# A two-layer 5x5 convolution: from 4-row to 6-row Winograd tiles, with part of the input transform on GpSimd and pair sums kept in PSUM

## The chip, the cores and the metric

The kernel runs on one core of one Trainium2 chip. The metric is device microseconds of one execution of the program. A core has five engines that run their own instruction queues in order: TensorE (PE in the profile; PEld is its loading of weights), VectorE (DVE), ScalarE (ACT), GpSimd (POOL) and SyncE (SP), which here only issues DMAs. Data lies in DRAM, in SBUF (128 partitions) and in PSUM, where TensorE writes its products.

## The reference

Two layers, each adding to x a 5x5 convolution of the group-normalised x (reflect padding, 16 groups of 2 channels, mean and variance over the group's pixels):

```python
def _gn(v, G=16, eps=1e-5):
    g = v.reshape(B_, G, C_ // G, H_, W_)
    m = jnp.mean(g, axis=(2, 3, 4), keepdims=True)
    s = jnp.var(g, axis=(2, 3, 4), keepdims=True)
    return ((g - m) / jnp.sqrt(s + eps)).reshape(v.shape)

x = x + _L0_conv_ref(_gn(x), L0_conv_weight)
x = x + _L1_conv_ref(_gn(x), L1_conv_weight)
```

x is (8, 32, 252, 252) in fp32, the weights are (32, 32, 5, 5). The convolution is written with an FFT in the reference; it is an ordinary 5x5 convolution with reflected borders.

## The kernel before

**Layout.** Pixels are grouped into 2x2 blocks. A partition is one of 4 positions in the block times 32 channels, 128 in all, and an image becomes 126x126 blocks, padded to 128x128. The 5x5 convolution is then a 3x3 convolution over blocks with 128 input and 128 output partitions.

**Winograd along block rows.** Along the rows of blocks the kernel uses F(4,3): 4 output rows from 6 input rows, by 6 products instead of 12. Along the columns it does the 3 taps directly, as 3 matmuls that accumulate. A step takes a group of 16 block rows as NT = 4 tiles of TR = 4 rows; the last group of an image has 14 real rows. There are NG = 8 groups to an image, 2 layers and 8 images, so 128 steps. Phases go (image 0, layer 0), then in turn (b, layer 0) and (b-1, layer 1).

**One step.**
- `fetch` (SP) loads the raw rows of a group of layer 0 into one half of `xbuf`. `prepare` makes g, the group's 18 block rows with their padding: for layer 0 with two big ScalarE copies (L131) and three small ones, for layer 1 with one DMA from `scratch` (L126).
- `transform` (VectorE) makes the six inputs v0 to v5 of the products from g: ab (L333), v1 and v2 (L342, L343), c (L345), v3 and v4 (L346, L347), and v0 and v5 in one tile (L349).
- `conv` runs six products, each 3 matmuls of 504 columns (4 tiles of 126) into one PSUM bank (L375), in the order 1, 2, 3, 4, 0, 5. ScalarE copies products 1 and 3 to SBUF (a1 with the offset, L390; a3, L398), so that each VectorE instruction has one operand in PSUM. VectorE forms s1 and d1 (L394, L395) and s2 and d2 (L402, L403), in SBUF, and from these the 4 rows of y (L404, L405, L408 to L412).
- y of the step before goes out during this step: for layer 0 `to_scratch` (padding copies, DMAs) and `output_sums` (two ScalarE activations that sum), for layer 1 `to_output` (four ScalarE copies L451, DMAs).

**Statistics and matrices.** `input_chunk` and `input_sums` sum the next image's input in 8 chunks; `collect`, `averages`, `variance`, `scales` make the group norm; `scale_matrices` scales the layer's matrices u by it on ScalarE, `add_own` adds the residual x (an identity) to them on VectorE, and `find_offset` makes the bias. The unscaled matrices of both layers stay in SBUF; they are made at the start by `load_taps`, `transform_taps` (GpSimd, L167 to L178) and `make_matrices` (ScalarE, L200).

**Order.** The schedule is by hand: each engine executes its instructions as the program emits them. In iteration i of the main loop come: fetch of step i+3, chunk loads, variance and collect where due, `transform` of step i+1, scales where due, then `conv` of step i with `after_1` (prepare of step i+2), `after_3` (output of step i-1, chunk sums) and `after_4` (add_own). So VectorE runs transform(i+1), conv(i), transform(i+2), conv(i+1) and so on. Tiles rotate over a fixed number of buffers in each pool: a new tile waits until the last user of the tile whose buffer it takes has ended; `ps_conv` has 7 PSUM banks.

Of the kernel before, what the change touches and what calls it, by code (L numbers as in the profile page):

```python
# [42 lines left out]
P = 128  # L44
# [4 lines left out]
TR = 4  # L49
NT = 4  # L50
GR = TR * NT
NG = PB // GR
NF = 6
# [3 lines left out]
def tile_conv_preact_x2(ctx: ExitStack, tc: tile.TileContext, x: bass.AP, w0: bass.AP, w1: bass.AP, out: bass.AP):  # L57
# [7 lines left out]
    prep = ctx.enter_context(tc.tile_pool(name="prep", bufs=1))  # L65
    upool = ctx.enter_context(tc.tile_pool(name="upool", bufs=2))
    xpool = ctx.enter_context(tc.tile_pool(name="xpool", bufs=1))
    spool = ctx.enter_context(tc.tile_pool(name="spool", bufs=3))
    gpool = ctx.enter_context(tc.tile_pool(name="gpool", bufs=2))
# [4 lines left out]
    opool = ctx.enter_context(tc.tile_pool(name="opool", bufs=1))  # L74
    small = ctx.enter_context(tc.tile_pool(name="small", bufs=3))
    dram = ctx.enter_context(tc.tile_pool(name="dram", bufs=3, space=bass.MemoryType.DRAM))
    ps_conv = ctx.enter_context(tc.tile_pool(name="ps_conv", bufs=7, space=bass.MemoryType.PSUM))
    ps_stat = ctx.enter_context(tc.tile_pool(name="ps_stat", bufs=1, space=bass.MemoryType.PSUM))
# [10 lines left out]
    xbuf = xpool.tile([P, GR + 2, W], F32, tag="x", name="x")  # L89
    fetched = 0  # L90

    def fetch(b: int, l: int, T: int):
# [4 lines left out]
        nr = min(GR + 2, PB - GR * T)  # L97
        half = fetched % 2
        fetched += 1
        for pr in range(2):  # L100
            t = xbuf[quads[2 * half + pr]]

            runs, pads = [], []
            for k in range(nr):
                h = 2 * (GR * T + k) + pr - 1
                if 0 <= h < H:
                    runs.append(k)
                else:
                    pads.append((k, {-1: 1, H: H - 2, H + 1: H - 3, H + 2: 2}[h]))
            first = 2 * (GR * T + runs[0]) + pr - 1  # L110
            nc.sync.dma_start(
                t[:, runs[0] : runs[-1] + 1, :], x[b, :, first : first + 2 * len(runs) - 1 : 2, :]
            )
            for k, h in pads:
                nc.sync.dma_start(t[:, k, :], x[b, :, h, :])
        xt[b, T] = xbuf[halves[half]]

    def prepare(b: int, l: int, T: int):

        nr = min(GR + 2, PB - GR * T)  # L120
        g = gpool.tile([P, GR + 2, PB], F32, tag="g", name=f"g_{b}_{l}_{T}")
        gt[b, l, T] = g
        if nr < GR + 2:
            nc.gpsimd.memset(g[:, nr:, :], 0.0)
        if l:
            nc.sync.dma_start(g[:, :nr, :], scratch[b][:, GR * T : GR * T + nr, :])  # L126
            return
        t = xt.pop((b, T))
        h0, h1 = halves
        for pc in range(2):  # L130
            nc.scalar.copy(g[halves[pc], :nr, 1 - pc : 1 - pc + NB], t[:, :nr, 1 - pc : W : 2])  # L131
        nc.scalar.copy(g[h0, :nr, 0 : PB : PB - 1], g[h0, :nr, 1 : NB : NB - 2])
        for dst, src in ((126, 125), (127, 1)):
            nc.scalar.copy(g[h1, :nr, dst : dst + 1], g[h1, :nr, src : src + 1])  # L134
# [3 lines left out]
    raw, total = [], []  # L138

    def load_taps(l: int, w: bass.AP):  # L140

        t = prep.tile([P, 2, 3, K, C], F32, tag=f"taps{l}", name=f"taps{l}")
        nc.vector.memset(t, 0.0)
        for pc in range(2):
            for pr in range(2):
                for rp in range(2):
# [4 lines left out]
                    nc.scalar.dma_start(  # L151
                        t[quad(pc, pr), rp, lo : lo + n], w[:, first : first + 2 * n - 1 : 2, :, :]
                    )
        return t

    def transform_taps(l: int, t: bass.AP):

        r = prep.tile([P, NF, 2, K, C], F32, tag="rows", name=f"rows{l}")
        s = prep.tile([P, 2, K, C], F32, tag="rsum", name=f"rsum{l}")
# [6 lines left out]

# [3 lines left out]
        v.tensor_scalar(both(1), both(1), -1.0 / 6, None, ALU.mult)  # L170
        v.tensor_scalar(rf[0], t2, 4.0, None, ALU.mult)
        v.tensor_add(rf[0], rf[0], t0)
        v.tensor_scalar(rf[5], t1, 2.0, None, ALU.mult)
        v.tensor_add(rf[3], rf[0], rf[5])
        v.tensor_sub(rf[4], rf[0], rf[5])
        v.tensor_scalar(both(3), both(3), 1.0 / 24, None, ALU.mult)
        v.tensor_scalar(rf[0], t0, 0.25, None, ALU.mult)
        v.tensor_copy(rf[5], t2)  # L178
        return r

    def sum_taps(l: int, t: bass.AP):

        sums = prep.tile([P, C], F32, tag="sums", name=f"sums{l}")
        nc.vector.tensor_reduce(sums, t.rearrange("p r a k o -> p o (r a k)"), axis=AX.X, op=ALU.add)
        tot = const.tile([P, 4, C], F32, tag=f"total{l}", name=f"total{l}")
        for q in range(4):
            nc.vector.tensor_scalar(tot[:, q, :], sums, 0.25, None, ALU.mult)
        total.append(tot.rearrange("p q o -> p (q o)"))

    def make_matrices(l: int, r: bass.AP):  # L190
        u = const.tile([P, NF, 3, 2, 2, C], F32, tag=f"u{l}", name=f"u{l}")
        nc.gpsimd.memset(u, 0.0)
        for pc in range(2):
            for cp in range(2):
# [4 lines left out]
                for rp in range(2):  # L199
                    nc.scalar.copy(  # L200
                        u[halves[pc], :, lo : lo + n, 1 - cp, 1 - rp, :],
                        r[halves[pc], :, rp, first : first + 2 * n - 1 : 2, :],
                    )
        raw.append(u.rearrange("p f b c r o -> p (f b c r o)"))
# [4 lines left out]
    def make_own():  # L209
        coef = ((1 / 4, -1 / 6, -1 / 6, 1 / 24, 1 / 24, 0.0), (0.0, -1 / 6, 1 / 6, 1 / 12, -1 / 12, 0.0))  # L210
        for pc in range(2):
            for pr in range(2):
                for f in range(NF):
                    nc.gpsimd.tensor_scalar(
                        own[quad(pc, pr), f, :], ident[quad(pc, pr), halves[pc]], coef[1 - pr][f], None, ALU.mult
                    )
# [5 lines left out]
    def make_averages():  # L222
        for l, pattern in enumerate(("p (q g e) -> p g q e", "p (g q e) -> p g q e")):
            kinds = {"q": 4, "e": 2}
            member = const.tile([P, C // 2], F32, tag=f"member{l}", name=f"member{l}")
            nc.vector.tensor_reduce(member, ident.rearrange(pattern, **kinds), axis=AX.XY, op=ALU.add)
            nc.vector.tensor_scalar(member, member, 1.0 / COUNT, None, ALU.mult)
            a = const.tile([P, 4, C // 2, 2], F32, tag=f"avg{l}", name=f"avg{l}")
            for q in range(4):
                for e in range(2):  # L230
                    nc.gpsimd.tensor_copy(a[:, q, :, e], member)
            avg.insert(0, a.rearrange("p q g e -> p (q g e)"))
# [4 lines left out]
    def sum_slots(b: int, l: int):  # L237
        if (b, l) not in sums:
            sums[b, l] = small.tile([P, 2, NG], F32, tag="sums", name=f"sums_{b}_{l}")
# [17 lines left out]
    def output_sums(b: int, T: int, y: bass.AP):  # L257
        rows = min(GR, NB - GR * T)
        st = sum_slots(b, 1)
        view = y[:, 0 : rows * PB].rearrange("p (r k) -> p r k", k=PB)[:, :, 1 : 1 + NB]  # L260
        junk = spool.tile([P, GR, NB], BF16, tag="junk", name=f"junk_{b}_{T}", bufs=1)
        nc.scalar.activation(junk[:, :rows], view, AF.Identity, accum_out=st[:, 0, T : T + 1])  # L262
        nc.scalar.activation(junk[:, :rows], view, AF.Square, accum_out=st[:, 1, T : T + 1])  # L263
# [6 lines left out]
    def averages(b: int, l: int):  # L270

        pm = ps_stat.tile([P, 2], F32, tag="pstat", name=f"pm_{b}_{l}")
# [29 lines left out]
    ut, offset = {}, {}  # L302

    def scale_matrices(b: int, l: int, first: bool = False):
        u = upool.tile([P, NF, 3, P], F32, tag="u", name=f"u_{b}_{l}")
        flat, r = u.rearrange("p f b m -> p (f b m)"), norm[b, l][:, 0:1]
        if first:
            nc.vector.tensor_scalar(flat, raw[l], r, None, ALU.mult)
        else:
            nc.scalar.activation(flat, raw[l], AF.Identity, scale=r)  # L310
        ut[b, l] = u
# [6 lines left out]
    def find_offset(b: int, l: int):  # L318
        po = ps_stat.tile([P, 1], F32, tag="pstat", name=f"po_{b}_{l}")
# [5 lines left out]
    vt = {}  # L325

    def transform(b: int, l: int, T: int):
        g = gt.pop((b, l, T))
        n = f"{b}_{l}_{T}"
        v = nc.vector  # L330
        ab = apool.tile([P, NT, TR, PB], F32, tag="ab", name=f"ab_{n}")
        flat = ab.rearrange("p t r k -> p (t r k)")
        v.scalar_tensor_tensor(  # L333
            flat,
            g[:, 0:GR, :].rearrange("p r k -> p (r k)"),
            -4.0,
            g[:, 2 : GR + 2, :].rearrange("p r k -> p (r k)"),
            ALU.mult,
            ALU.add,
        )  # L340
        vs = [vpool.tile([P, NT, PB], F32, tag=f"v{k}", name=f"v{k}_{n}") for k in range(1, 5)]
        v.tensor_add(vs[0], ab[:, :, 2, :], ab[:, :, 1, :])  # L342
        v.tensor_sub(vs[1], ab[:, :, 2, :], ab[:, :, 1, :])  # L343
        c = apool.tile([P, NT, 2, PB], F32, tag="c", name=f"c_{n}")
        v.tensor_sub(c.rearrange("p t r k -> p t (r k)"), rows_of(g, 3), rows_of(g, 1))  # L345
        v.scalar_tensor_tensor(vs[2], c[:, :, 0, :], 2.0, c[:, :, 1, :], ALU.mult, ALU.add)  # L346
        v.scalar_tensor_tensor(vs[3], c[:, :, 0, :], -2.0, c[:, :, 1, :], ALU.mult, ALU.add)  # L347
        v05 = vpool.tile([P, NT, 2, PB], F32, tag="v05", name=f"v05_{n}")
        v.tensor_sub(  # L349
            v05.rearrange("p t r k -> p t (r k)"),  # L350
            ab[:, :, 2:4, :].rearrange("p t r k -> p t (r k)"),
            ab[:, :, 0:2, :].rearrange("p t r k -> p t (r k)"),
        )
        vt[b, l, T] = [v05[:, :, 0, :], *vs, v05[:, :, 1, :]]

    def rows_of(g: bass.AP, j: int):

        return g[:, j - 1 : j - 1 + GR, :].rearrange("p (t r) k -> p t r k", r=TR)[:, :, 1:3, :].rearrange(
            "p t r k -> p t (r k)"
        )  # L360
# [236 lines left out]
```

## Time and profile before

| what | value |
|---|---|
| time, median of 3 runs | 2029.58 us (2028.38 to 2029.70) |
| profiled execution | 2029.54 us, of which the span from first to last instruction is 2027.8 us |
| granted TensorE clock, mean | 0.997 |
| VectorE, largest groups | ab L333 292.2 us in 128, 2283 ns each; v0 and v5 L349 156.5 us, 1223 ns each |
| ScalarE, largest groups | o L451 283.3 us in 256; g L131 290.2 us in 128 |
| GpSimd | work in the start only, and 16 memsets of 0.31 us later |
| DMA | 346.77 MB, mean 171 GB/s |
| first matmul of a product | at 54.96 us |

A group of the page is a line of the program with an engine and an operation: the total busy time, the mean duration of one in ns, the idle time of the engine just before them and what ended it. The timeline gives start, duration, engine, line, operation, output <- inputs. Records of neighbouring instructions on one engine may overlap; so the distance from start to start tells what an instruction costs its engine.

### The profile page before, as it was taken

The numbers are of one execution on the slowest core, as the hardware profiler recorded it, in microseconds if no ns is written. First come the engines' busy times: TensorE is split into PE (matmuls) and PEld (weight loads), VectorE is DVE, ScalarE is ACT, GpSimd is POOL, SyncE is SP. The second block draws the span as 40 slices with busy tenths as digits, with TensorE's granted clock in tenths as the row PEclk, the third lists the DMA queues.
The fourth block names the chain that finished last, engine by engine and source line by source line (L and its number), as shares of the span: only waits on it lengthen the run. The fifth ranks groups of instructions, "written<-read, shape, count | busy, mean of one in ns | idle before, by whom it ended". The sixth has DMA issues, their size and how long they took to land.

```text
span 2027.8 us, 15748 instructions
## 1 busy us (share of the span) xinstructions
PE 1960.0 (97%) x4672; PEld 879.9 (43%) x4672; DVE 1799.5 (89%) x2392; ACT 1331.0 (66%) x1589; POOL 48.5 (2%) x88
## 2 busy tenths in 40 slices
PE   0999999999999999999999999999999999999997
PEld 0444444444444444444444444444444444444443
DVE  5889999998998999899898998999899898998995
ACT  5898757677667776677666776658666677533433
POOL 7100000000000000000000000000000000000000
PEclk9999999999999999999999999999999999999999
DMA  8877757867567757677666776676766776454553
GB/s 239 213 177 152 149 170 213 210 133 153 186 215 181 155 132 216 208 173 147 161 204 198 156 160 164 201 208 149 160 181 193 210 145 140 118 160 129 145 156 79
DMA packets 179285, 346.77 MB, mean 171 GB/s; under 512 B 14080, under 2 KB 154624, under 8 KB 163840
## 3 DMA queue, kind: packets, MB, share of 16 engines
q1 hardware_dynamic: 177664, 344.95, 66.9%
q10 hardware_dynamic: 1536, 0.82, 0.2%
q8 instruction: 37, 0.61, 0.1%
q14 instruction: 48, 0.39, 0.1%
HBM read 213.58 MB, written 132.14 MB: 170 GB/s over the span
## 4 chain that ended last, share of the span: by engine, by line
PE 90%; ACT 4%; DVE 2%; DMA 2%; issue 1%; SPq 0%; ACTq 0%; DVEq 0%
PE m L375 90%; ACT g L131 1%; DMA sx<-in_x_dram 1%; DMA taps<-in_L_conv_weight_dram 1%; ACT sx L255 1%; ACT sx L254 1%; DVE ab L333 0%; ACT u L200 0%; ACT o L451 0%; ACT junk L262 0%; ACT junk L263 0%; DVE y L404 0%; DVE y L405 0%; DVE v L342 0%; DVE d L403 0%
## 5 line engine op out<-in xcount | busy, mean ns | idle before, releaser
L375 PE MATMUL m<-v,u 128*128 128x504 f32 x4608 | 1958.2, 587 | 2.6 <-ACT u L310 1.5
L375 PEld LDWEIGHTS m<-v,u 128*128 128x128 f32 x4608 | 869.8, 189 | 1067.4 <-issue 1014.8
L333 DVE SCALAR_TENSOR_TENSOR ab<-g 128x2048 f32<-128x2048 f32 x128 | 292.2, 2283 | 3.0 <-ACT g L134 3.0
L390 ACT ACTIVATE a<-m,off 128x504 f32<-128x504 f32 x128 | 87.1, 680 | 312.5 <-PE m L375 312.2
L131 ACT COPY g<-x 64x2268 f32<-64x2268 f32 (+1 forms) x128 | 290.2, 2267 | 2.4
L451 ACT COPY o<-y 64x1008 f32<-64x1008 f32 (+1 forms) x256 | 283.3, 1107 | 7.4 <-issue 4.0
L398 ACT COPY a<-m 128x504 f32<-128x504 f32 x128 | 74.1, 579 | 276.5 <-PE m L375 275.0
L349 DVE TENSOR_TENSOR v<-ab 128x1024 f32<-128x1024 f32 x128 | 156.5, 1223 | 0.0
L411 DVE TENSOR_TENSOR d<-m,d 128x504 f32<-128x504 f32 x128 | 87.1, 681 | 77.5 <-PE m L375 77.5
L345 DVE TENSOR_TENSOR c<-g 128x1024 f32<-128x1024 f32 x128 | 155.8, 1217 | 0.0
L402 DVE TENSOR_TENSOR s<-m,a 128x504 f32<-128x504 f32 x128 | 87.1, 680 | 58.3 <-PE m L375 46.5
L255 ACT ACTIVATE sx<-sx 128x2016 f32<-128x2016 f32 x64 | 118.8, 1857 | 21.9 <-DMA taps<-in_L_conv_weight_dram 12.9
L263 ACT ACTIVATE junk<-y 128x2016 bf16<-128x2016 f32 x64 | 118.9, 1858 | 2.0
L262 ACT ACTIVATE junk<-y 128x2016 bf16<-128x2016 f32 x64 | 118.9, 1858 | 1.6
L254 ACT ACTIVATE sx<-sx 128x2016 f32<-128x2016 f32 (+1 forms) x58 | 107.1, 1847 | 4.0 <-DMA sx<-in_x_dram 3.3
L408 DVE TENSOR_TENSOR s<-m,s 128x504 f32<-128x504 f32 x128 | 87.4, 683 | 12.6 <-DVE y L405 0.5
L404 DVE SCALAR_TENSOR_TENSOR y<-d,d 128x504 f32<-128x504 f32 x128 | 87.4, 683 | 12.1 <-ACT o L451 8.0
L342 DVE TENSOR_TENSOR v<-ab 128x512 f32<-128x512 f32 x128 | 89.1, 696 | 4.4
L346 DVE SCALAR_TENSOR_TENSOR v<-c 128x512 f32<-128x512 f32 x128 | 88.5, 692 | 4.4
L405 DVE SCALAR_TENSOR_TENSOR y<-s,s 128x504 f32<-128x504 f32 x128 | 87.4, 683 | 4.4
L409 DVE TENSOR_TENSOR y<-s,s 128x504 f32<-128x504 f32 x128 | 87.4, 683 | 4.4
L412 DVE SCALAR_TENSOR_TENSOR y<-d,d 128x504 f32<-128x504 f32 x128 | 87.4, 683 | 4.4
(65 smaller groups left out, 747.8 us busy)
## 6 DMA issues: line engine op xcount, KB each, us to landing
g<-scratch SPq DMA_DIRECT2D x56, 1152.0 KB, 8.7
out_dram<-o SPq DMA_DIRECT2D x240, 252.0 KB, 3.7
x<-in_x_dram SPq DMA_DIRECT2D x104, 567.0 KB, 8.0
scratch<-y SPq DMA_DIRECT2D x224, 256.0 KB, 3.6
sx<-in_x_dram SPq DMA_DIRECT2D x56, 1008.0 KB, 7.3
g<-scratch SPq DMA_DIRECT2D x8, 1024.0 KB, 10.0
scratch<-y SPq DMA_DIRECT2D x32, 224.0 KB, 2.8
sx<-in_x_dram SPq DMA_DIRECT2D x8, 882.0 KB, 7.3
```

Source lines behind the costliest of these rows:

```text
L131: nc.scalar.copy(g[halves[pc], :nr, 1 - pc : 1 - pc + NB], t[:, :nr, 1 - pc : W : 2])
L254: nc.scalar.activation(t, t, AF.Identity, accum_out=st[:, 0, c : c + 1])
L255: nc.scalar.activation(t, t, AF.Square, accum_out=st[:, 1, c : c + 1])
L262: nc.scalar.activation(junk[:, :rows], view, AF.Identity, accum_out=st[:, 0, T : T + 1])
L263: nc.scalar.activation(junk[:, :rows], view, AF.Square, accum_out=st[:, 1, T : T + 1])
L333: v.scalar_tensor_tensor(flat, g[:, 0:GR, :].rearrange("p r k -> p (r k)"), -4.0, g[:, 2 : GR + 2, :].rearrange("p r k -> p (r k)"), ALU.mult,
L342: v.tensor_add(vs[0], ab[:, :, 2, :], ab[:, :, 1, :])
L345: v.tensor_sub(c.rearrange("p t r k -> p t (r k)"), rows_of(g, 3), rows_of(g, 1))
L346: v.scalar_tensor_tensor(vs[2], c[:, :, 0, :], 2.0, c[:, :, 1, :], ALU.mult, ALU.add)
L349: v.tensor_sub(v05.rearrange("p t r k -> p t (r k)"), ab[:, :, 2:4, :].rearrange("p t r k -> p t (r k)"), ab[:, :, 0:2, :].rearrange("p t ...
L375: nc.tensor.matmul(ps, u[:, f, b3, :], vs[f][:, :, 2 - b3 : 2 - b3 + NB], start=(b3 == 0), stop=(b3 == 2),)
L451: nc.scalar.copy(o[halves[s], :n, 1 - pc : W : 2], yr[halves[pc], s * half : s * half + n, 1 : 1 + NB])
```

## The change

- F(6,3) instead of F(4,3): 6 output rows from 8 input rows by 8 products. A group is 18 block rows, NT = 3 tiles of TR = 6; 7 groups cover the 126 rows exactly. 112 steps, each with 24 matmuls of 378 columns.
- The input transform begins with two additions over (128 x 1536) elements, a and e, and ends with one over 768 (`ends`, which makes v0 and v7); in the main loop GpSimd does these three, a and e one step ahead of the rest. VectorE does e := e - 17/4 low, v1, v2, p, v3, v4, q, v5, v6. a, e, p and q have one buffer each.
- The sums and differences of products 3 and 4, and of 5 and 6, are written by VectorE over the products in PSUM. ScalarE copies products 1, 3 and 5. y is written in two passes of six scalar_tensor_tensor, and then two additions for products 0 and 7.
- PSUM is one pool of 8 banks. Unscaled matrices lie in DRAM (`stored`) and are loaded into one of two SBUF buffers before each phase; the scaling is in place. prepare and fetch run one step earlier. Output of a step is split over `after_3` and `after_5`. The taps are loaded on SP's queue, those of layer 1 later than before. At the start all chunks are summed by VectorE and squared by ScalarE.

```diff
-TR = 4
-NT = 4
+TR = 6
+NT = 3
...
-NG = PB // GR
-NF = 6
+IR = GR + 2
+NG = NB // GR
+NF = 8
...
-    ps_conv = ctx.enter_context(tc.tile_pool(name="ps_conv", bufs=7, space=bass.MemoryType.PSUM))
-    ps_stat = ctx.enter_context(tc.tile_pool(name="ps_stat", bufs=1, space=bass.MemoryType.PSUM))
+    psum = ctx.enter_context(tc.tile_pool(name="psum", bufs=8, space=bass.MemoryType.PSUM))
...
+    def differences(v, b: int, l: int, T: int):
+
+        g = gt[b, l, T]
...
+        a = apool.tile([P, NT, 4, PB], F32, tag="a", name=f"a_{n}")
+        e = apool.tile([P, NT, 4, PB], F32, tag="e", name=f"e_{n}")
+        v.tensor_sub(rows(a), rows(high[:, :, 1:5]), rows(low[:, :, 1:5]))
+        at[b, l, T] = a, e
+        return lambda: v.tensor_add(rows(e), rows(high[:, :, 2:6]), rows(low[:, :, 0:4]))
...
+        stt = lambda o, i0, c, i1: v.scalar_tensor_tensor(o, i0, c, i1, ALU.mult, ALU.add)
+        stt(rows(e), rows(low[:, :, 2:6]), -17 / 4, rows(e))
+        v.tensor_add(vs[0], e[:, :, 2], e[:, :, 1])
+        v.tensor_sub(vs[1], e[:, :, 2], e[:, :, 1])
+        yield
+        stt(rows(p), rows(a[:, :, 0:2]), -1 / 4, rows(a[:, :, 2:4]))
+        stt(vs[2], p[:, :, 0], 2.0, p[:, :, 1])
+        stt(vs[3], p[:, :, 0], -2.0, p[:, :, 1])
+        stt(rows(q), rows(a[:, :, 0:2]), -4.0, rows(a[:, :, 2:4]))
+        stt(vs[4], q[:, :, 0], 0.5, q[:, :, 1])
+        stt(vs[5], q[:, :, 0], -0.5, q[:, :, 1])
+        vt[b, l, T] = [v07[:, :, 0], *vs, v07[:, :, 1], v07]
+        yield
+
+    def ends(v, b: int, l: int, T: int):
+
+        a, e = at.pop((b, l, T))
+        v.tensor_sub(rows(vt[b, l, T].pop()), rows(e[:, :, 2:4]), rows(e[:, :, 0:2]))
...
         m4 = product(4)
-        s2, d2 = temp("s2"), temp("d2")
-        v.tensor_add(s2, m4, a3)
-        v.tensor_sub(d2, a3, m4)
...
+        v.tensor_sub(m3, a3, m4)
+        v.tensor_add(m4, m4, a3)
+        for j, c in enumerate((1.0, 2.0, 4.0, 8.0, 16.0, 32.0)):
+            stt(yo[j], m3 if j % 2 else m4, c, d1 if j % 2 else s1)
+        m5 = product(5)
+        a5 = temp("a5", 2)
+        nc.scalar.copy(a5, m5)
+        after_5()
+        m6 = product(6)
+        v.tensor_sub(m5, a5, m6)
+        v.tensor_add(m6, m6, a5)
+        for j, c in enumerate((1.0, 1 / 2, 1 / 4, 1 / 8, 1 / 16, 1 / 32)):
+            stt(yo[j], m5 if j % 2 else m6, c, yo[j])
         m0 = product(0)
+        v.tensor_add(yo[0], m0, yo[0])
+        m7 = product(7)
+        v.tensor_add(yo[5], m7, yo[5])
...
+        for p in mid.get(i, []):
+            nc.sync.dma_start(ut[p], stored[p[1]])
...
         if i + 1 < N:
-            transform(*steps[i + 1])
+            for _ in transform(*steps[i + 1]):
+                pass
+        if i + 2 < N:
+            rest = differences(nc.gpsimd, *steps[i + 2])
+        if i + 1 < N:
+            ends(nc.gpsimd, *steps[i + 1])
+        if i + 2 < N:
+            rest()
```

`stt` is scalar_tensor_tensor: output = (first input x constant) + second input. At the start the changed kernel runs, in this order on SP: three chunk loads, the taps of layer 0, the fetch of group 0, the other chunks, the store of the raw matrices, the fetches of groups 1 and 2 and the taps of layer 1; and on GpSimd: the own matrices, the taps of layer 0, a memset of a matrix buffer, a and e of step 1, the 18 instructions for the taps of layer 1, and then a, ends and e of the steps.

## The prediction

> **What bounds the kernel now.** I read the page first: the busy shares, the chain that ended last, the costliest groups.
>
> ```profile
> PE 1960.0 (97%) x4672; PEld 879.9 (43%) x4672; DVE 1799.5 (89%) x2392; ACT 1331.0 (66%) x1589; POOL 48.5 (2%) x88
> PE 90%; ACT 4%; DVE 2%; DMA 2%; issue 1%; SPq 0%; ACTq 0%; DVEq 0%
> L375 PE MATMUL m<-v,u 128*128 128x504 f32 x4608 | 1958.2, 587 | 2.6 <-ACT u L310 1.5
> L411 DVE TENSOR_TENSOR d<-m,d 128x504 f32<-128x504 f32 x128 | 87.1, 681 | 77.5 <-PE m L375 77.5
> ```
>
> TensorE is busy 97% of the span and carries 90% of the chain: it is the bound, idle 2.6 us in 4608 records (two for each fp32 matmul). VectorE (DVE) stands at 89%, and its idle time waits for TensorE. So VectorE is second by only 8 points, and any change that moves work from matmuls to elementwise must be costed there.
>
> Next the timeline of VectorE in a steady step (start, duration, line). The start-to-start distances price its instructions, because neighbours overlap.
>
> ```profile
> 315.00 0.69 DVE L346 SCALAR_TENSOR_TENSOR v<-c 128x512 f32<-128x512 f32 x1
> 315.61 0.68 DVE L347 SCALAR_TENSOR_TENSOR v<-c 128x512 f32<-128x512 f32 x1
> ...
> 317.94 0.67 DVE L395 TENSOR_TENSOR d<-a,m 128x504 f32<-128x504 f32 x1
> 318.53 0.67 DVE L402 TENSOR_TENSOR s<-m,a 128x504 f32<-128x504 f32 x1
> ...
> 319.82 0.68 DVE L404 SCALAR_TENSOR_TENSOR y<-d,d 128x504 f32<-128x504 f32 x1
> 320.54 0.68 DVE L405 SCALAR_TENSOR_TENSOR y<-s,s 128x504 f32<-128x504 f32 x1
> ```
>
> An instruction that does not depend on the one before starts 0.59 us after it (L395 to L402); L405 starts 0.72 us after L404 although its inputs were ready for over 1 us. Both write rows of the same y tile, and the program's order has L405 wait for VectorE itself: writes to interleaved rows of y run strictly one after another.
>
> Last the timeline of the start, the only place where GpSimd (POOL) and VectorE work on SBUF together.
>
> ```profile
> 19.30 0.86 POOL L175 TENSOR_TENSOR rows<-rows 128x320 f32<-128x320 f32 x1
> ...
> 40.86 0.69 DVE L347 SCALAR_TENSOR_TENSOR v<-c 128x512 f32<-128x512 f32 x1
> 40.95 1.88 ACT L255 ACTIVATE sx<-sx 128x2016 f32<-128x2016 f32 x1
> 41.07 1.20 POOL L168 TENSOR_TENSOR rows<-rsum,taps 128x320 f32<-128x320 f32 x1 [3.13 <-ACT u L200]
> 41.47 1.89 DVE L349 TENSOR_TENSOR v<-ab 128x1024 f32<-128x1024 f32 x1
> 42.23 1.84 POOL L169 TENSOR_TENSOR rows<-rsum,taps 128x320 f32<-128x320 f32 x1
> ```
>
> Alone, the GpSimd addition of 320 elements takes 0.86 us, and L349 1.22 us (the mean of its group is 1223 ns). Side by side they take turns. L168 waits until L347 ends at 41.55, then holds for 0.72 us; L349, whose record had already begun, loses 0.67 us. L169 then waits for L349. A GpSimd instruction that waits gets its turn at the next boundary between VectorE instructions, even ahead of one that is next in VectorE's queue.
>
> **TensorE after the change.** 128 steps of 18 matmuls become 112 of 24. In the tail 42 records take 17.91 us, so 0.426 us for 504 columns; scaled by columns, 378 come to 0.32. A step is 24 x 2 x 0.32 = 15.4 us, 1720 us in all against 1958. If TensorE stayed the bound, the gain would be some 240 us.
>
> **VectorE after the change, per step.** Price by elements at 0.96 per ns: the rows of 512, 1024 and 2048 elements, 0.69, 1.22 and 2.28 us, lie on that slope. From the distances above: 384 elements, independent, 0.605 - 0.133 = 0.472 us; 378 independent 0.462, dependent 0.715 - 0.131 = 0.584; 768 with a dependent successor (L345 to L346 1.245) 0.978; 1536 likewise (L333 to L342 2.32) 1.787.
> - Transform: e 1.79, p and q 2 x 0.98, six v 6 x 0.47: 6.6 us. Two additions and the ends (v0 and v7) went to GpSimd.
> - Conv: 20 instructions of 378. Twelve scalar_tensor_tensor write y rows, then two additions write y again, and each of these waits for the one before. Fourteen distances are dependent, six are not: 14 x 0.584 + 6 x 0.462 = 10.95 us. The four sums into PSUM are taken at the same price: a PSUM operand shows none (L402 680 ns, the SBUF-only L404 683). A PSUM output has no row; the bounds are 0 and another dependent wait, 4 x 0.12 = 0.5 us a step.
>
> That is 17.5 us against 15.4 for TensorE: VectorE becomes the bound even with GpSimd free of charge. Before, it was 14.6 us (310.22 to 324.82), for 16 rows instead of 18.
>
> **GpSimd per step.** a (1536), ends (768), e (1536), in this order. The row of 320 gives a's hold: 0.72 x 4.8 = 3.46 us if all of it streams, or, with 0.21 us fixed (1.01 and 1.81 us for 320 and 640 elements of TENSOR_SCALAR), 0.21 + 0.51 x 4.8 = 2.66. I take the middle, 3.06. Further bounds use other slopes behind the 0.72: a memset's 0.88 ns per element gives 1.8, TENSOR_SCALAR's 2.5 ns gives 3.8. All three together need some 8 us of a step of 17 to 20, so GpSimd is no bound itself.
>
> Where it hurts: a has one buffer, so a of step i+2 may start when q of step i+1, its last reader, has ended. That is inside VectorE's transform, with v5 and v6 still to come, both with two SBUF inputs. v5 starts 0.04 us after q (dependent neighbours in the rows above), GpSimd 0.07 us (its L231 after L227 in the start); so v5 goes first, a takes the next boundary, and v6 stands still for 3.06 - 0.05 = 3.0 us. Then come conv's instructions, each with one PSUM operand; beside them I count GpSimd as free. The nearest row is the one-input TENSOR_REDUCE L252 at 14.29, which kept 2.25 us beside GpSimd. Behind v6 stand the whole conv and the next transform; TensorE, 5 us ahead per step, hides nothing of it. A step is then 20.5 us.
>
> No row has a PSUM-fed VectorE instruction beside a GpSimd read. [...] The page "GPSIMD Engine Reference" (section "Performance versus the Vector engine") gives 4497 ns for an addition of 2048 elements; an estimate from it is 3.4 us for a, and the sum would be about 35 us higher.
>
> **Rest.** Per phase change VectorE also runs a reduction, three and six tiny instructions of 0.19 us and two add_own of 0.60: 3.1 us, fifteen times, 47 us; TensorE hid them before. ScalarE: two prepare copies of 2520 elements (2.27 us for 2268, so 2.5), three PSUM copies under 0.6, sums of 2.1, about 12 us a step, hidden by 20. DMA bytes stay; g and y have three and two buffers, so loads land a step early.
>
> Start: the first product comes near 55 us as now (the taps on SP's queue and a longer GpSimd transform of them against input sums that no longer wait for ACT's queue). But on SP the fetch of group 1 stands behind the store of the raw matrices, which waits for ACT's make_matrices, near 47: it lands near 57, prepare ends near 63, GpSimd's a and e near 70. The second taps' 18 instructions (19 us by the rows of the first, some 4 more for conflicts) then stand in GpSimd's queue ahead of a, ends and e for step 2: transform of step 2 starts near 101 instead of 88.
>
> **Sum.** 101 + 110 transforms x 6.6 = 726 + 111 convs x 10.95 = 1215 + 109 stalls x 3.0 = 327 + 47 + tail 10 (last VectorE record to the end was 8.8; four copies get 1.1 longer) = 2426 us of span. The profiled execution's span is 2027.8 and its time 2029.54, so 2428; the median of the runs is 2029.58, no shift.
>
> **Rivals.**
> - No stall: VectorE wins every turn. For it: v6 is independent and already queued. Against: L349 was too and lost. 2428 - 327 = about 2100.
> - Two stalls: a is taken before v5 and the ends before v6. The two releases lie 0.03 us apart. The ends hold 0.72 x 2.4 = 1.7 or 1.4 us; another 1.53 x 109 = 167: 2595.
> - PSUM-fed instructions block as well: all three GpSimd holds fall on VectorE, 4.6 more a step: 2930. The reduction row speaks against it.
> - Clock: the first matmuls after the idle start come 0.84 us apart instead of 0.42 until 58.4. TensorE would now idle some 5 us a step, in gaps up to 2.6 us (m3 waits for its PSUM slot). At half rate throughout a step is 30.7 us: 3520. Half rate for some of it is hidden.
> - Faster: VectorE's fixed part between instructions vanishes, elements alone remaining: 12936 / 0.96 = 13.5 us instead of 17.5. With the stall, 2428 - 111 x 4.0 = about 1980. It decides from 3.6 us saved a step. For it: neighbours overlap by 0.08 us; against: every distance above.
>
> **How the numbers follow.** One stall 0.68, two 0.15, none 0.08, PSUM blocked 0.03, clock 0.03, faster 0.03. The likeliest gives 2428. Its own range is 2290 (hold 1.8) to 2520 (3.8, and 20 for the start). To leave no more than 2 in 10 out I take in the two stalls and the error of 0.4 us a step in the prices: 2240 to 2640. A measurement can tell 0.2%, 4 us, from no change: faster 0.03, same 0.01, slower 0.96.
>
> **What would show it.** VectorE near 95% busy, TensorE near 70%; v6 at about 3.5 us a piece and v5 at 0.56; y writes 0.58 apart; a of 3.1 to 3.4 us right behind q; steps of 20.5 us. Wrong if v6 keeps 0.56, or if the y writes overlap, or if TensorE's rows stretch.

## The result, and the profile after

| kernel | median of the runs | profiled span | TensorE clock granted, mean |
|---|---|---|---|
| before | 2029.64 us (2028.38 to 2030.71) | 2027.8 us | 0.997 |
| after | 2537.77 us (2537.61 to 2538.44) | 2536.0 us | 0.885 |

The ratio is 1.2504 (95% interval 1.2483 to 1.2526): the change made the kernel 25% slower. The forecast of 2428 us is 110 us under the median, which lies inside the range of 2240 to 2640.

The page of the changed kernel: busy time and share of each engine, the chain that ended last, three groups of instructions.

```profile
PE 1946.3 (77%) x5440; PEld 1096.3 (43%) x5440; DVE 2402.5 (95%) x3473; ACT 1303.9 (51%) x1537; POOL 1081.4 (43%) x410
DVE 66%; PE 13%; issue 8%; DMA 6%; ACT 5%; SPq 1%; DVEq 0%; ACTq 0%
L390 PE MATMUL m<-v,u 128*128 128x378 f32 x5376 | 1935.0, 521 | 406.7 <-DVE d L411 288.7
L344 POOL TENSOR_TENSOR a<-g 128x1536 f32<-128x1536 f32 x111 | 418.7, 3772 | 1392.4 <-DVE q L358 1303.0
L358 DVE SCALAR_TENSOR_TENSOR v<-q 128x384 f32<-128x384 f32 x224 | 469.3, 2136 | 3.9
```

VectorE and TensorE have changed places. VectorE is busy 95% and carries 66% of the chain; TensorE idles 406.7 us, most of it behind d1 (L411), which frees PSUM slots. One group stands out by its mean: v5 and v6 ("v<-q") take 2136 ns each, and the same operation on the same shape takes 555 ns as v3 and v4. GpSimd's a (L344) waits for q, and its own mean, 3772 ns, is too long: e of GpSimd, of the same shape, has a mean of 3448.

A steady step on the timeline of the changed kernel (start, duration, engine, line; "x2" is two records in a row, in brackets the idle time before and what ended it):

```profile
1199.83 1.75 DVE L358 SCALAR_TENSOR_TENSOR e<-g,e 128x1536 f32<-128x1536 f32 x1
...
1204.48 0.95 DVE L358 SCALAR_TENSOR_TENSOR q<-a 128x768 f32<-128x768 f32 x1
1205.47 4.28 DVE L358 SCALAR_TENSOR_TENSOR v<-q 128x384 f32<-128x384 f32 x2
1205.58 3.76 POOL L344 TENSOR_TENSOR a<-g 128x1536 f32<-128x1536 f32 x1 [11.55 <-DVE q L358]
1209.30 2.13 POOL L375 TENSOR_TENSOR v<-e 128x768 f32<-128x768 f32 x1
1209.68 0.54 DVE L410 TENSOR_TENSOR s<-m,a 128x378 f32<-128x378 f32 x1
...
1211.51 3.45 POOL L346 TENSOR_TENSOR e<-g 128x1536 f32<-128x1536 f32 x1
...
1213.97 0.55 DVE L403 SCALAR_TENSOR_TENSOR y<-m,s 128x378 f32<-128x378 f32 x1
1214.56 0.55 DVE L403 SCALAR_TENSOR_TENSOR y<-m,d 128x378 f32<-128x378 f32 x1
1215.03 0.55 DVE L427 TENSOR_TENSOR m<-a,m 128x378 f32<-128x378 f32 x1
...
1216.07 3.48 DVE L403 SCALAR_TENSOR_TENSOR y<-m,y 128x378 f32<-128x378 f32 x6
...
1219.66 0.55 DVE L432 TENSOR_TENSOR y<-m,y 128x378 f32<-128x378 f32 x1
1220.31 0.55 DVE L434 TENSOR_TENSOR y<-m,y 128x378 f32<-128x378 f32 x1
1220.78 1.75 DVE L358 SCALAR_TENSOR_TENSOR e<-g,e 128x1536 f32<-128x1536 f32 x1
```

Read it from e to e: the step is 20.95 us. v5 starts at 1205.47; a is ready 0.11 us later, waits out v5 and goes ahead of v6. v5 and v6 together last 4.28 us; where nothing disturbs them (v3 and v4) the pair lasts 1.03. So v6 stands still for 3.25 us, and conv with it. Then e of GpSimd (1211.51 to 1214.96) runs beside conv, whose instructions have one operand in PSUM, and these keep 0.55 us, the rows of y 0.585 us apart. L427, which does not touch y, starts only 0.47 us after the last row of a pass.

The other place is the step in which a phase changes. The same view, later in that step's transform:

```profile
215.65 2.12 POOL L375 TENSOR_TENSOR v<-e 128x768 f32<-128x768 f32 x1
216.03 0.15 DVE L306 RECIPROCAL inv<-std 128x1 f32<-128x1 f32 x1
216.21 1.57 DVE L307 TENSOR_TENSOR fix<-inv 128x1 f32<-128x1 f32 x1
217.81 0.16 DVE L308 TENSOR_TENSOR fix<-fix,var 128x1 f32<-128x1 f32 x1
217.84 3.42 POOL L346 TENSOR_TENSOR e<-g 128x1536 f32<-128x1536 f32 x1
218.00 0.15 DVE L309 TENSOR_SCALAR fix<-fix 128x1 f32<-128x1 f32 x1
218.19 3.08 DVE L310 TENSOR_TENSOR mr<-inv,fix 128x1 f32<-128x1 f32 x1
```

These are five of the six instructions of `scales`, on one element in each partition; the last, L311, follows at 221.31, when e is over, and takes 0.16 us. L308 and L309 take 0.16 and 0.15 us; L307 lasts until GpSimd's ends are over (217.78), and L310 until GpSimd's e is (221.27). Both read two SBUF tensors. L308 does too, but it began in the gap between two GpSimd instructions.

### The profile page after: what moved, and what is told of

Same layout as the page of the kernel before. It is cut to its first block, busy times and chain, and to the rows that moved or that the text cites. A ratio compares the mean times of both kernels' runs of the same rounds, so it can differ in the third digit from the quotient of the medians.

```text
span 2536.0 us, 18838 instructions
## 1 busy us (share of the span) xinstructions
PE 1946.3 (77%) x5440; PEld 1096.3 (43%) x5440; DVE 2402.5 (95%) x3473; ACT 1303.9 (51%) x1537; POOL 1081.4 (43%) x410
## 4 chain that ended last, share of the span: by engine, by line
DVE 66%; PE 13%; issue 8%; DMA 6%; ACT 5%; SPq 1%; DVEq 0%; ACTq 0%
DVE y L403 19%; DVE v L358 16%; PE m L390 13%; DVE e L358 5%; DVE p L358 3%; DVE q L358 3%; DMA scratch<-y 3%; DVE d L411 2%; DVE mr L310 2%; DVE y L432 2%; DVE s L410 2%; DVE v L360 2%; DVE m L427 2%; DMA sx<-in_x_dram 2%; DVE v L361 2%
## 5 line engine op out<-in xcount | busy, mean ns | idle before, releaser
L390 PE MATMUL m<-v,u 128*128 128x378 f32 x5376 | 1935.0, 521 | 406.7 <-DVE d L411 288.7
L390 PEld LDWEIGHTS m<-v,u 128*128 128x128 f32 x5376 | 1082.1, 205 | 1243.5 <-DVE d L411 328.5
L344 POOL TENSOR_TENSOR a<-g 128x1536 f32<-128x1536 f32 x111 | 418.7, 3772 | 1392.4 <-DVE q L358 1303.0
L358 DVE SCALAR_TENSOR_TENSOR v<-q 128x384 f32<-128x384 f32 x224 | 469.3, 2136 | 3.9
L403 DVE SCALAR_TENSOR_TENSOR y<-m,y 128x378 f32<-128x378 f32 x672 | 370.5, 551 | 23.1
L346 POOL TENSOR_TENSOR e<-g 128x1536 f32<-128x1536 f32 x111 | 382.7, 3448 | 8.6
L468 ACT COPY o<-y 64x1134 f32<-64x1134 f32 x224 | 278.0, 1241 | 175.6 <-DVE y L434 159.3
L144 ACT COPY g<-x 64x2520 f32<-64x2520 f32 x112 | 280.4, 2503 | 14.0 <-DMA x<-in_x_dram 12.0
L375 POOL TENSOR_TENSOR v<-e 128x768 f32<-128x768 f32 x111 | 236.4, 2130 | 7.7 <-DVE e L358 7.7
L275 ACT ACTIVATE junk<-y 128x2268 bf16<-128x2268 f32 x112 | 234.7, 2095 | 1.4
L269 ACT ACTIVATE sx<-sx 128x2016 f32<-128x2016 f32 x64 | 118.8, 1857 | 19.4 <-DVE sums L266 17.1
```

The source lines that it names most:

```text
L144: nc.scalar.copy(g[halves[pc], :, 1 - pc : 1 - pc + NB], t[:, :, 1 - pc : W : 2])
L269: nc.scalar.activation(t, t, AF.Square, accum_out=st[:, 1, c : c + 1])
L275: nc.scalar.activation(junk, view, (AF.Identity, AF.Square)[k], accum_out=st[:, k, T : T + 1])
L344: v.tensor_sub(rows(a), rows(high[:, :, 1:5]), rows(low[:, :, 1:5]))
L346: return lambda: v.tensor_add(rows(e), rows(high[:, :, 2:6]), rows(low[:, :, 0:4]))
L358: stt = lambda o, i0, c, i1: v.scalar_tensor_tensor(o, i0, c, i1, ALU.mult, ALU.add)
```

## The experiments

Each was timed beside the kernel before on the same chip (2028.9 to 2029.9 us). Times are medians, ratios are to the kernel before.

**1. a behind v6.** If q lies in a's tile, the next a takes a buffer whose last readers are v5 and v6, and GpSimd waits for v6.

```diff
-        a = apool.tile([P, NT, 4, PB], F32, tag="a", name=f"a_{n}")
+        a = apool.tile([P, NT, 6, PB], F32, tag="a", name=f"a_{n}")
...
-        v.tensor_sub(rows(a), rows(high[:, :, 1:5]), rows(low[:, :, 1:5]))
+        v.tensor_sub(rows(a[:, :, 0:4]), rows(high[:, :, 1:5]), rows(low[:, :, 1:5]))
...
-        q = apool.tile([P, NT, 2, PB], F32, tag="q", name=f"q_{n}")
+        q = a[:, :, 4:6]
```

> q is kept in two extra rows of a's tile, so the next a waits for v6, the last reader of q, instead of for q; nothing else differs from the changed kernel (2538 us). Theory: the stall is the turn that GpSimd's a takes between v5 and v6. v5 and v6 together fall from 4.27 us to 1.03, a, ends and e run beside the conv, whose instructions have one SBUF input and keep 0.55 us each; 109 x 3.25 = 354 us less, some 10 us given back where the six tiny scale instructions of a phase change now meet a and the ends instead of the ends and e: 2190 us. Rival: PSUM-fed instructions are blocked as well, so the hold of 3.4 us only moves into the conv: above 2500 us, and s1 or d1 of some 4 us in place of v6.

Measured: 2223.70 us, ratio 1.0956 (1.094 to 1.0972). The timeline of a step:

```profile
1212.92 0.95 DVE L358 SCALAR_TENSOR_TENSOR a<-a 128x768 f32<-128x768 f32 x1
1213.91 1.03 DVE L358 SCALAR_TENSOR_TENSOR v<-a 128x384 f32<-128x384 f32 x2
1214.85 0.54 DVE L410 TENSOR_TENSOR s<-m,a 128x378 f32<-128x378 f32 x1
1215.01 3.46 POOL L344 TENSOR_TENSOR a<-g 128x1536 f32<-128x1536 f32 x1 [8.92 <-DVE v L358]
...
1215.77 0.55 DVE L418 TENSOR_TENSOR m<-a,m 128x378 f32<-128x378 f32 x1
```

v5 and v6 are back at 1.03 us, a takes 3.46 us and covers the first seven or so instructions of conv at no cost to them, outputs to PSUM (L418) included. The step is 17.69 us, so one boundary cost 3.25 us a step. The price of 2190 was missed by 34 us, mostly at the phase changes: three two-input instructions of `scales` now wait for GpSimd, instead of two.

```profile
L310 DVE TENSOR_TENSOR mr<-inv,fix 128x1 f32<-128x1 f32 x16 | 37.1, 2317 | 0.6
L308 DVE TENSOR_TENSOR fix<-fix,var 128x1 f32<-128x1 f32 x16 | 36.9, 2306 | 0.6
L307 DVE TENSOR_TENSOR fix<-inv 128x1 f32<-128x1 f32 x16 | 28.5, 1781 | 0.6
```

Those are groups of experiment 1. Their busy time is 102.5 us; in the changed kernel it was 23.7 + 2.5 + 46.3 = 72.5 us. That is 30 us more, where 10 had been allowed for. Another 10 us lie in the two steps after a change into layer 1, where VectorE waits for ScalarE's output copies (L468, 7.7 us in all) and for a product (2.6 us); the last 4 are rounding, since the terms of the expectation add up to 2194.

**2. `scales` inside the transform.** Its six instructions go to the `yield` ahead of p, v3 to v6 and q, where GpSimd has nothing to do yet.

```diff
-            for _ in transform(*steps[i + 1]):
-                pass
+            parts = transform(*steps[i + 1])
+            next(parts)
+            for p in late.get(i, []):
+                scales(*p)
+            next(parts)
...
-        for p in late.get(i, []):
-            scales(*p)
```

> The six tiny instructions of scales at a phase change stand inside the transform, after v2, where GpSimd is idle, instead of between the transform and the conv. Theory: two of them have two SBUF inputs and wait there for the ends and for e (1.57 us and 3.08 us instead of 0.16): 15 x 4.33 = 65 us less, 2473 us. Rival: the 110 us by which the changed kernel lies above the forecast come from TensorE, whose granted clock fell to 0.885, so that products are late: no change, 2538 us within 5.

Measured: 2472.67 us, ratio 1.2183 (1.2165 to 1.2201): 65.1 us less than the changed kernel, as expected. The step of a phase change is 23.42 us instead of 27.74, and the groups of experiment 2 are:

```profile
L307 DVE TENSOR_TENSOR fix<-inv 128x1 f32<-128x1 f32 x16 | 2.5, 159 | 0.6
L310 DVE TENSOR_TENSOR mr<-inv,fix 128x1 f32<-128x1 f32 x16 | 2.5, 159 | 0.6
```

The granted clock stayed low, at 0.897, and yet the whole 65 us came back. The rival, that the clock makes the difference, falls.

**3. No GpSimd.** a, ends and e on VectorE, in the same places (a and e of step 1 too).

```diff
-            rest = differences(nc.gpsimd, *steps[i + 2])
+            rest = differences(nc.vector, *steps[i + 2])
...
-            ends(nc.gpsimd, *steps[i + 1])
+            ends(nc.vector, *steps[i + 1])
```

> a, ends and e of the main loop are done by VectorE, in the same places; GpSimd does nothing in the loop. Theory (a hold of GpSimd costs VectorE 3.25 us a step and the additions on VectorE would cost 1.67 + 0.88 + 1.67 = 4.2 us): 0.95 x 110 = 105 us more, 65 us less at the phase changes, some 5 to 10 us less at the start: 2570 us. Rival (the offload costs more than it takes off, because GpSimd slows VectorE in other places too): clearly below 2538 us.

Measured: 2583.94 us, ratio 1.2731 (1.2712 to 1.275). The step is 22.02 us, against 17.69 in experiment 1, where GpSimd does the same work without the stall. So the offload takes 4.33 us a step off VectorE, and by the turns that GpSimd takes it gives back 3.25 of these and the 65 us at the phase changes: it gains 46 us in all. That is 14 us more than was expected, because a step rose by 1.07 us and not by 0.95.

**4. Rows of y apart.** In the changed kernel the six rows of a tile are interleaved in y, and every write to y waits for the write before it. Here y is laid out row by row over the tiles, so that neighbouring writes go to separate stretches. One pass of ScalarE (L441), which replaces the sum of y, brings it back to the old order for `to_scratch`; the copies of `to_output` go tile by tile.

```diff
-        yr = y[:, 0 : GR * PB].rearrange("p (t r k) -> p t r k", r=TR, k=PB)
-        yo = [yr[:, :, j, 1 : 1 + NB] for j in range(TR)]
+        yr = y[:, 0 : GR * PB].rearrange("p (r t k) -> p r t k", r=TR, k=PB)
+        yo = [yr[:, j, :, 1 : 1 + NB] for j in range(TR)]
```

> y is laid out with the row inside the tile outermost, so the six rows written by the passes lie in separate stretches; the sum over y of layer 0 writes a copy in the old order, from which the store goes, and the output copies take the rows in pieces. The waits of each y write for the one before are gone from the program, except behind m4 and m6. Theory: twelve distances fall from 0.585 to 0.465 us, 1.45 us a step, 111 x 1.45 = 160 us: 2375 us. Rival: the distance of 0.585 is set by VectorE itself when it writes a strided output from a PSUM input, whatever the program waits for: 2538 us within 10.

Measured: 2352.03 us, ratio 1.1588 (1.1569 to 1.1608), 185.7 us less than the changed kernel. The timeline of experiment 4:

```profile
1212.28 0.54 DVE L403 SCALAR_TENSOR_TENSOR y<-m,s 128x378 f32<-128x378 f32 x1
1212.74 0.54 DVE L403 SCALAR_TENSOR_TENSOR y<-m,d 128x378 f32<-128x378 f32 x1
...
1219.35 0.54 DVE L432 TENSOR_TENSOR y<-m,y 128x378 f32<-128x378 f32 x1
1219.81 0.54 DVE L434 TENSOR_TENSOR y<-m,y 128x378 f32<-128x378 f32 x1
```

The records are as long as before, but 0.46 us apart instead of 0.585. The step fell by 1.67 us, where 1.45 was expected: L434 had come 0.65 us behind L432, and comes 0.46 behind it now. The rival, that VectorE itself needs this time after a strided write, falls too: already in the changed kernel L427 starts 0.47 us after such a write.

**5. Experiments 1 and 2 together.**

> The edits of e1_a_after_v6 and e2_scales_early together. In e1 the tiny instructions of scales met a, the ends and e and took 102.5 us in the profile (1.78, 2.31 and 2.32 us each where 0.16 is their length). Theory: both stalls are turns lost to GpSimd and nothing else is wrong with the offload: 2224 - 95 = 2129 us. Rival: something beyond these two places is left, so the two edits do not add: above 2150 us.

Measured: 2166.61 us, ratio 1.0674 (1.0658 to 1.069); 37 us above what was expected, on the rival's side. The steps are 17.70 us and `scales` is cheap, but one more instruction with two SBUF inputs has met GpSimd. Experiment 5, a phase change:

```profile
203.37 3.79 POOL L346 TENSOR_TENSOR e<-g 128x1536 f32<-128x1536 f32 x1
203.90 3.81 DVE L324 TENSOR_TENSOR u<-u,own 64x512 f32<-64x512 f32 x1
```

It is the second of the two `add_own` instructions, 0.69 us in the changed kernel. Its group grew from 21.8 us in experiment 1 to 68.7, by 46.9 us; the steps after the phase changes, which no longer wait, give 10 us of that back, and what is left is the miss. In experiment 1, where `scales` still held VectorE back, the pair began 2 us after e's end (207.50 against 205.54); with `scales` out of the way VectorE reaches it while e still runs.

**6 to 8. Towards a faster version.** Experiment 6 is 5 with 4. Experiment 7 adds an order in which no instruction of VectorE directly follows the one whose result it needs (e, p, v1, v2, q, v3 to v6; the rows of y as 1, 0, 3, 2, 5, 4 and 1, 0, 5, 2, 3, 4). Experiment 8 adds, at the start, the fetch of group 1 and the taps of layer 1 before the store of the raw matrices, and the GpSimd work on the taps ahead of a of step 1.

```diff
-        for j, c in enumerate((1.0, 2.0, 4.0, 8.0, 16.0, 32.0)):
+        for j, c in ((1, 2.0), (0, 1.0), (3, 8.0), (2, 4.0), (5, 32.0), (4, 16.0)):
...
+        if c == 5:
+            fetch(*steps[1])
+            load_taps(1, w1, taps_at[:, 1])
```

> e5 and e4_y_rows_outer together. Theory: VectorE is still the bound at 17.5 - 1.7 = 15.8 us a step, and the 186 us that e4 saved are saved again: 1943 us, faster than the kernel before. Rival: TensorE, 15.4 us a step at full clock but held by PSUM banks that the passes release late and by a lower granted clock, takes over: 2000 us or more, with VectorE waiting for products.

> e6 with the order on VectorE changed so that no instruction comes straight behind the one that makes its input: e, p, v1, v2, q, v3 to v6, and the passes over y start with row 1. Theory: seven distances lose 0.12 us each, 0.8 us a step, VectorE comes to 15.0 us and TensorE's 15.4 become the bound: 101 + 111 x 15.4 + 10 + some us at the phase changes, 1840 to 1900 us. Rival: TensorE is already the bound in e6 or its banks are: no gain over e6.

> e7 with the fetch of group 1 and the taps of layer 1 put ahead of the store of the raw matrices on SP's queue, and the second taps' transform ahead of a and e of step 1 on GpSimd. Theory: the transform of step 2 starts some 14 us earlier: 14 us less than e7. Rival: the start is hidden by later slack: no change.

| experiment | median | ratio (95% interval) | usual step | step of a phase change | granted clock |
|---|---|---|---|---|---|
| 6 | 1991.85 us | 0.9813 (0.9797 to 0.983) | 16.03 us | 22.2 us | 0.956 |
| 7 | 1928.46 us | 0.9500 (0.9486 to 0.9514) | 15.39 us | 21.85 us | 0.968 |
| 8 | 1920.36 us | 0.9461 (0.9447 to 0.9475) | 15.39 us | 21.9 us | 0.970 |

All three beat the kernel before, experiment 6 by less than 2%, and all three missed their expectation. Experiment 6 was expected at 1943 before experiment 5 had run, so it carries that miss of 37 us; it is 49 us above, and `add_own` grew by another 8.6 us (77.3 us in its group). Experiment 7 came 28 us above the upper end of its range; `add_own` stands at 79.6 us there. VectorE is busy 97% of its span there and TensorE 92%, both with a step near 15.4 us. The expectation had TensorE as the bound; but VectorE's waits that end with a matmul sum to 3.2 us, so VectorE still was, at 15.39 us a step where 15.0 had been expected. Experiment 8 gained 8 us of the 14 expected. The transform of step 2 starts at 88.6 us instead of 100.7, but early steps became longer (18.29 and 16.07 us) while VectorE waited for ScalarE's a3.

**9. `add_own` at the end of the step.** Experiment 8 with one more edit:

```diff
-            for p in late.get(i, []):
-                add_own(*p)
...
         done = step, conv(*step, after_1, after_3, after_5)
+        for p in late.get(i, []):
+            add_own(*p)
```

> e8 with one thing moved: the two instructions that add the own matrices to u (L324, two SBUF inputs, 64x512) come behind the last additions into y instead of between the fifth and the sixth product. There GpSimd's e, which ended 0.2 us before the next transform in the usual steps of e8, should be over. Theory (the pair's second instruction waits for GpSimd's e): both take some 0.7 us alone, the phase-change step goes from 21.9 to some 18 us, and the total falls by 3.1 to 3.9 us x15, 47 to 59 us, to 1861-1873 us. Rival (what stands behind u on TensorE decides): the next step's first product can't begin before the pair has ended, TensorE falls behind, VectorE waits for the first additions of that step, and what is gained in one step is lost in the next: above 1905 us.

Measured: 1913.24 us, ratio 0.9428 (0.9412 to 0.9443). The gain is 7 us, far from 47. The timeline of experiment 9 at a phase change:

```profile
307.37 1.40 DVE L324 TENSOR_TENSOR u<-u,own 64x512 f32<-64x512 f32 x2
308.10 22.37 PE L390 MATMUL m<-v,u 128*128 128x378 f32 x64 [3.88 <-DVE u L324]
308.80 1.76 DVE L358 SCALAR_TENSOR_TENSOR e<-g,e 128x1536 f32<-128x1536 f32 x1
...
317.24 0.56 DVE L418 TENSOR_TENSOR m<-a,m 128x378 f32<-128x378 f32 x1 [1.22 <-PE m L390]
```

One half of the theory came true: the pair takes 1.40 us, and the step here, a change into layer 1, 17.9 instead of 21.8 us. But the rival decided, with its mechanism and its total (above 1905 us): TensorE, which may not touch u before, idles 3.88 us, and VectorE then waits for it. After each of the eight changes into layer 1 the next step takes 16.8 to 17.1 us instead of 15.4, and after six of them a later step is 1.3 to 1.5 us longer as well, so 1.5 to 3.0 of the 3.96 us gained are given back. At the seven changes into layer 0 the step falls less, to 18.7 to 19.2 us, and the next two take some 18.0 and 16.1 us instead of 15.4 each: that gives back more than was gained. A wait removed at one place was met again at the next: `scales` behind a (1), `add_own` behind e (5), TensorE behind `add_own` (9). It is the fastest kernel of the study all the same.

## Why the prediction was right, and what was mis-sized

**Right.** The direction and the mechanism: VectorE became the bound (95% busy, 95 predicted; TensorE 77%, 70 predicted), v6 lost the boundary to a, exactly one stall a step. Experiment 1 shows the stall by removing it: v6 returns to its price, and the steps shorten by 3.25 us. The term for serial writes of y stands too (0.585 us measured, 0.584 predicted), and experiment 4 shows that the waits between interleaved writes, not the elements, make it. The transform of step 2 starts at 100.91 us, 101 predicted; the early term in it was off, the first product came at 50.6 instead of 55 us, but GpSimd's queue decided, as said.

PSUM-fed instructions ran free beside GpSimd, so the rival at 2930 falls; outputs to PSUM, which no row had shown, cost nothing extra (L418 to L419 0.46 us apart). The Trainium skill (page "SBUF — State Buffer", section "Who interferes with whom") says that a VectorE instruction with two SBUF inputs contends with a GpSimd instruction that reads SBUF, and that one with at most one does not, unless it runs in a mode that uses two ports, as tensor_scalar can. The trace agrees: the PSUM-fed instructions keep 0.54 to 0.55 us beside a, ends and e, and v6, L307 and L310, with two SBUF inputs, stand still. The prediction had counted two-input instructions alone; but in the start L194, a TENSOR_SCALAR with one SBUF input that takes 0.23 us at 14.46, lasts 2.03 us from 67.94, until GpSimd's e is over at 69.93. No run shows the mode that it ran in.

**Mis-sized, 44 us: "A step is then 20.5 us".** The step was 20.95 us, 0.40 us over the sum of its terms (6.6 + 10.95 + 3.0 = 20.55), in 109 steps. Stall: "3.06 - 0.05 = 3.0 us" was 3.25; a takes 3.46 us alone, the upper value of its first pair of bounds, and holds some 3.3 us from the end of v5 (1206.02) to its own (1209.34), where 3.06, the middle, was taken. Conv: 11.10 us (1209.68 to 1220.78) instead of 10.95, because the two last additions into y (L432, L434) came 0.66 and 0.65 us behind the instruction before them, where 0.584 had been taken; why these two take longer stays open. The estimate of 3.4 us that the prediction made from a page of the Trainium skill ("GPSIMD Engine Reference", section "Performance versus the Vector engine") was the better one: a took 3.46 us where nothing stood in its way.

**Mis-sized, 65 us: "Per phase change VectorE also runs ... 3.1 us, fifteen times, 47 us".** The instructions were counted, but priced as if alone. Two of the six of `scales` waited for GpSimd's ends and e: 1.57 + 3.08 us instead of 2 x 0.16, so 4.33 us more, fifteen times. The prediction had the case for it in its own rows (L349, with two SBUF inputs, lost 0.67 us to GpSimd) and applied it to v6 alone; it did not ask what else with two SBUF inputs VectorE runs while GpSimd is at work, however small. Experiment 2 shows these 65 us by moving the six instructions. Together 44 + 65 = 109 us, of the 110 that were missing.

**The clock, rival at 3520.** The granted clock did fall, to 0.885, and TensorE's mean record is 521 ns there against 491 in experiment 7 at 0.968. "Wrong if TensorE's rows stretch" was thus half met. It cost nothing: of all VectorE's waits in the changed kernel, only 0.7 us end with a matmul, one of the statistics, and experiment 2 gained its 65 us at a clock of 0.897. The stretched rows also account for TensorE's 77% busy instead of 70.

**Two stalls, no stall, faster.** The step shows one stall, of a at v6, and the ends come when conv runs. Without the stall the kernel takes 2223.70 us (experiment 1), above the rival's 2100 because of the phase changes (65 us, and 40 more that experiment 1 itself brought in and after them) and conv's 0.15 us a step. VectorE's fixed part between instructions shrank only where the program took its waits away (experiments 4 and 7).

## What to carry to other kernels

Here work moved to GpSimd was free for VectorE beside instructions with one operand in PSUM, and not beside those with two SBUF inputs: list each two-input instruction of every stage, the tiny ones of rare stages too, and ask which GpSimd instruction is queued at that moment. What that is worth: against no offload (experiment 3) the changed kernel gained 46 us, and experiment 5, with the same offload and two collisions fewer, 417 us. A single buffer decides by its last reader where GpSimd takes its turn, so one more reader at the right place can move the collision out. And where VectorE is the bound, instructions that write interleaved rows of one tile, or read the result of the one just before, paid about 0.12 us each here; experiments 4 and 7 took 1.67 and 0.64 us a step off in this way, together over half of the 4.33 us that the offload took off.

## What the runs showed of the hardware that was not expected

- A VectorE instruction on 128x1 elements with two SBUF inputs can take 3.08 us instead of 0.16, because a GpSimd addition of 1536 elements is running. The length of the blocked instruction played no part (L324 of 512 elements went from 0.69 to 3.81 us); what was left of GpSimd's did.
- GpSimd's additions waited too, and only for boundaries: a of 1536 elements took 3.46 us when it started beside conv and 3.76 when it had to wait for the end of v5.
- The mean granted clock went with how busy TensorE was: 0.885 in the changed kernel, 0.928, 0.944, 0.956 and 0.968 in experiments 1, 5, 6 and 7, with TensorE at 77, 83, 85, 90 and 92% busy. In the changed kernel and in experiments 1, 5 and 6 VectorE's waits that end with TensorE sum to under 5 us, so the lowered clock did not reach the time.
